# Softmax denominators in four column tiles, spread back by transfers, in a fused two-layer attention kernel

## The chip, the cores and the metric

The kernel runs on one core of a Trainium2 chip. The metric is the device time of one execution in microseconds; the number reported is the median of several. One profiled execution gives the trace from which all durations come.

## The reference

Two layers run one after the other on x, eight images of 512 channels and 32x32 = 1024 positions, all in float32. The change lies in the first layer. Cut to what matters here:

```python
h = _group_norm(x, gn_w, gn_b)                       # 32 groups of 16 channels
qkv = einsum('oc,bcn->bon', qkv_w, h) + qkv_b        # 8 heads of 64 channels
attn = einsum('bhdi,bhdj->bhij', q, k) * 64 ** -0.5
attn = softmax(attn, axis=-1)
out = einsum('bhij,bhdj->bhdi', attn, v)
out = einsum('oc,bcn->bon', proj_w, out) + proj_b
x = x + out
```

The second layer ranks the 1024 tokens of each image by their squared norm, normalizes the 256 largest and lets them attend to each other, writes the result back into the values, projects, and adds x again.

## The kernel before

**Tiling.** Layer 0 is cut into 64 units. A unit t is a pair of heads (p = t // 2, four pairs an image) and one half of the 1024 queries (512 of them), so eight units make an image b, and `at` = t % 8 is the unit's place in it. Keys lie on partitions: the scores of a unit come as eight tiles j of 128 keys by (2 heads x 512 queries). A softmax over keys is thus a reduction over partitions and over j.

**Steps of a unit.** Each is a small function, named in SLOT by a word:

- sc (L943): two matmuls, one per head, into a PSUM tile of two banks. keep (ACT, L951) copies it to SBUF (e); max (DVE, L957) folds it into a running maximum.
- turn (PE, L966): eight transposes of that maximum; neg (DVE, L971) reduces them to one negated maximum per query; spread (PE, L980) transposes it back over all partitions (ns).
- sub (DVE, L986) adds ns to e; exp (ACT, L989); add (POOL, L994) sums the eight e tiles into es, seven adds a unit; val (PE, L1002) multiplies e with v, two heads in two column tiles of 64, accumulated over the eight j into one bank (av).
- den (`total`, PE, L1015): ones times es, which sums the 128 partitions. Two matmuls, one per head, each with 64 columns of ones and 512 queries, so that each head's sum stands on the 64 partitions on which av has that head. take (ACT, L1023) copies the sums to ri; inv (DVE, L1027) takes the reciprocal; div (DVE, L1033) multiplies av with it into o.
- fill and empty: work of other units beside the attention: projections of q and k (L740), the v values (L761), the output projection of the image before (L779), each a group of matmuls into the one bank g, emptied by ACT or, for the output projection, by DVE (L786), with a store of the result and a load of the next residual rows on SP. A unit has three fills; a unit with `at` 1 to 4 has two more, of the output projection.

**What sets the order.** PE, DVE, ACT and POOL each run their instructions in the order in which the program names them; there is no scheduler for them. SLOT is that order, written out by hand: in the loop over t each word calls its step for unit t, with + for unit t+1 and - for unit t-1. The text is the same for every slot, and a step without work there is left out. SP, which issues the loads and stores, follows its own queue, in which a DMA behind a waiting one waits too. A loop with NORM and NORM1 hangs the group norm of the next image on words of SLOT: the statistics (L655), two small matmuls with gmat that sum over channel groups (`mean_sum` L660, `variance_sum` L678), their copies out (`mean_take` L665, `variance_take` L683), the factors, and the application (L699, four an image).

**Buffers.** PSUM has eight banks: two tiles of two banks (tag s) go round among the eight sc tiles, pt of turn and den; one tile of two banks is ns; one bank is av, one is g. A new tile of tag s waits until the readers of the tile two before it are done. In the first two units of an image den's second bank also takes the group-norm sums of the next image. av has one buffer, so the first val of a unit waits for div of the unit before.

**Around the end.** At t = UNITS-3 `load_layer1` puts x of image 0 and the weights of layer 1 (4 MB) on SP. The last slots also do layer 1's first steps (token rows, token values, importance counts), and `begin_layer1` (L1082) and `finish` (L1100) close layer 0 with the last den and the last output projections. Layer 1 has orders of its own (BATCH, END), which the change leaves alone.

Of the kernel before, what the change touches and what calls it, by code (L numbers as in the profile page):

```python
# [9 lines left out]
F32 = mybir.dt.float32  # L10
# [8 lines left out]
P = 128  # L19
B = 8  # L20
C = 512
N = 1024
CT = C // P
NB = N // P
NH = 2
HALF = N // NH
HEADS = 8
HD = 64
NPAIR = HEADS // 2
# [8 lines left out]
XT = 4  # L38
# [5 lines left out]


SLOT = """
take- sc0+ sc1+ spread inv- empty0 keep1+ fill1 keep0+ sub1 sub0 val6- exp1 sc2+ max1+
exp0 sc3+ sub3 div- empty1 sub7 sub4 fill2 keep2+ max3+ exp3 val0 max2+ val1 exp7 exp4
add1 add3 keep3+ add4 sub5 val3 sc4+ sc5+ empty2 fill3 exp5 val7 add7 empty3 sub2 keep5+
val5 max4+ val4 max5+ sub6 fill4 keep4+ empty4 add5 exp2 sc6+ max6+ exp6 sc7+ add2 keep6+  # L50
max7+ add6 keep7+ fill0+ turn+ den neg+ val2
"""


# [62 lines left out]
def attention_then_topk_attention(  # L117
# [18 lines left out]
    nc = tc.nc  # L136
# [33 lines left out]
    keep_pool = ctx.enter_context(tc.tile_pool(name="r1", bufs=2))  # L170
# [425 lines left out]
    def layer0():  # L596
        with ExitStack() as st:
# [6 lines left out]
            ap = st.enter_context(tc.tile_pool(name="ap", bufs=2))  # L604
# [90 lines left out]
            def norm_apply(b, c):  # L695
# [8 lines left out]


            NORM = {
                (-3, "max", 7): [(norm_stats, 0)], (-2, "div", 0): [(norm_stats, 1)],
                (-1, "div", 0): [(norm_stats, 2)], (0, "div", 0): [(norm_stats, 3)],
                (0, "neg", 0): [(mean_take,), (spread_of,)], (1, "neg", 0): [(variance_take,)],
                (2, "max", 7): [(norm_factors,)],  # L710
                (3, "sub", 5): [(norm_apply, c) for c in range(CT)],
            }

            NORM1 = {
                (-1, "max", 3): [(norm_stats, 0), (norm_stats, 1)],
                (-1, "max", 7): [(norm_stats, 2), (norm_stats, 3)],
                (3, "div", 0): [(norm_apply, 0)], (3, "sub", 5): [(norm_apply, 1)],
                (3, "sub", 6): [(norm_apply, 2)], (3, "max", 7): [(norm_apply, 3)],
            }

            def norms(t, name, j):
                for b in {t // (NPAIR * NH) + 1, (t + 3) // (NPAIR * NH) + 1}:
                    at = t - (b - 1) * NPAIR * NH
                    if 0 < b < B:
                        todo = NORM.get((at, name, j), [])
                        if b == 1 and name != "neg" and at != 2:
                            todo = NORM1.get((at, name, j), [])
                        for step, *which in todo:
                            step(b, *which)


            def project(p, which, hf):

                b, hp = divmod(p, NPAIR)
                all_ = (qs, ks)[which]
                ot = which * CT + hp

                def fill(pq):
                    for k in range(CT):
                        nc.tensor.matmul(  # L740
                            pq, wqkv[:, k, ts(ot, P)], hs[b][:, k, ts(hf, HALF)],
                            start=(k == 0), stop=(k == CT - 1),
                        )

                def empty(pq):
                    if hf == 0:
                        all_[p] = qp.tile([P, N], F32, tag="qk"[which], name=f"{'qk'[which]}_{p}")
                    nc.scalar.activation(
                        all_[p][:, ts(hf, HALF)], pq, AF.Identity, bias=bqkv[:, ot : ot + 1],
                    )  # L750

                return fill, empty
# [243 lines left out]
            def values(t, j):  # L996
# [4 lines left out]
                for hh in range(2):  # L1001
# [3 lines left out]
                        e[:, hh, :], start=(j == FIRST), stop=(j == LAST),  # L1005
                    )

            def total(t, _):
                den = ps_s.tile([P, 2, HALF], F32, tag="s", name=f"den_{t}")
                b, at = divmod(t, NPAIR * NH)  # L1010
                if b + 1 < B and at < 2:
                    (mean_sum, variance_sum)[at](b + 1, den[:, 1, :])
                es = sums.pop(t)
                for hh in range(2):
                    nc.tensor.matmul(  # L1015
                        den[HD * hh : HD * hh + HD, 0, :], ones0[:, :HD], es[:, hh, :],
                        start=True, stop=True,
                    )
                dens[t] = den

            def take(t, _):
                ri = ap.tile([P, HALF], F32, tag="ri", name=f"ri_{t}")
                nc.scalar.copy(ri, dens[t][:, 0, :])  # L1023
                dens[t] = ri

            def invert(t, _):
                nc.vector.reciprocal(dens[t], dens[t])  # L1027

            def divide(t, _):
                p, hf = divmod(t, NH)  # L1030
# [80 lines left out]
            with tc.manual_schedule(engines=ORDERED):  # L1111
                for c in range(CT):
                    norm_stats(0, c)
                mean_sum(0, ps_g.tile([P, HALF], F32, tag="g", name="pm_0"))
                mean_take(0)
                spread_of(0)
                variance_sum(0, ps_g.tile([P, HALF], F32, tag="g", name="pv_0"))
                variance_take(0)
                norm_factors(0)
                for c in range(CT):  # L1120
                    norm_apply(0, c)

                FIRST_STEPS = {
                    ("sc", 1): project(0, 0, 1), ("sc", 3): v_tokens(0, 0), ("sc", 5): v_tokens(0, 1),
                    ("keep", 0): "empty", ("keep", 3): "empty", ("keep", 4): "empty",
                }
                pending = []

                def first(step):
                    if step == "empty":  # L1130
                        end, pt = pending.pop(0)
                        end(pt)
                    else:
                        pool, tag = ((ps_g, "g"), (ps_a, "av"))[len(firsts) % 2]
                        firsts.append(step)
                        pt = pool.tile([P, HALF], F32, tag=tag, name=f"first_{len(firsts)}")
                        step[0](pt)
                        pending.append((step[1], pt))

                firsts = []  # L1140
                for step in (
                    project(0, 1, 0), project(0, 0, 0), "empty", project(0, 1, 1), "empty", "empty",
                ):
                    first(step)
                for t in range(-1, UNITS + 1):
                    b, at = divmod(t, NPAIR * NH)
                    if t == -1:
                        hs[1] = load_x(1)
                    if 0 <= t and at == CT + 1 and b + 2 < B:
                        hs[b + 2] = load_x(b + 2)  # L1150
                    if b == B - 1 and at == 0:
                        pair = tiles["pair"] = xp.tile([P, CT, N], F32, tag="x0", name="pair")
                        for i, src in enumerate((wvT, woT)):
                            nc.sync.dma_start(
                                pair[:, :, ts(i, C)], src.rearrange("(k p) o -> p k o", p=P)
                            )
                    if t == 2:
                        constants()
                    if t == UNITS - 3:
                        load_layer1()  # L1160
                    if 0 < b < B and 1 <= at <= CT:
                        for hf in range(NH):
                            load_residual(b - 1, at - 1, hf)
                    if t == UNITS - 1:
                        for mt in range(3):
                            load_residual(B - 1, mt, 0, spare(f"xr_last_{mt}")[:, :HALF])
                    for name, ahead, j in order:
                        if 0 <= t + ahead < UNITS and (name, t) != ("den", UNITS - 1):
                            STEPS[name](t + ahead, j)
                        if t == -1 and (name, j) in FIRST_STEPS:  # L1170
                            first(FIRST_STEPS[name, j])
                        norms(t, name, j)
                        if t == UNITS - 4 and name == "empty" and j == 4:
                            fill(t, 5)
                        if t == UNITS - 4 and (name, j) == ("exp", 6):
                            empty(t, 5)
                        if t == UNITS - 1 and (name, j) == ("fill", 1):
                            also(token_rows(1))
                            also(token_rows(2))
                    if t == UNITS - 1:  # L1180
                        begin_layer1()
                finish()
# [48 lines left out]
```

## Time and profile before

| | us |
|---|---|
| median of 3 runs | 2642.75 (2640.84 to 2644.28) |
| the profiled execution | 2641.48 |
| its span (first to last instruction) | 2639.8 |
| one image in the steady stretch | 258 |
| an ordinary unit of three fills (den to den, 1019.29 to 1047.90) | 28.6 |
| layer 0 ends, layer 1 begins at about | 2156 |
| reciprocal, DVE, 64 times | 3.352 each |
| copy of the sums, ACT, 64 times | 0.586 each |
| add, POOL, 448 times | 2.38 each |

How to read the lines further down: a group line has the line of the program, engine, operation, output and inputs, shape and count; then busy time and mean duration in ns; then the idle time ahead of it and what ended it. A timeline line has start, length, engine, line and operation, and in brackets the idle time ahead. A line of the table by stretch has the stretch, its length, and for PE, PE's weight loads, DVE, ACT and POOL the busy time (and the count); then the granted TensorE clock as a share of full speed, the share of the DMA engines' time, and GB/s.

TensorE's matmuls are pipelined, and the ends of its records are modelled. The start of one group to the start of the next is the better measure of what a group costs.

### The profile page before, as it was taken

The page shows a single profiled execution, that of the slowest core. Times are in us where ns is not written, and L with a number is a line of the kernel's source. Part 1 is how long each engine was busy: PE and PEld are TensorE (multiplying, and loading weights), DVE is VectorE, ACT ScalarE, POOL GpSimd, SP SyncE. Part 2 cuts the span into 40 slices and gives each one's busy share as a digit, 9 for nine tenths or more (in the row PEclk, how much of TensorE's full clock was granted, in tenths as well). Part 3 has the DMA queues.
Part 4 walks back from the last instruction along what each step waited for, and adds up shares of the span by engine and source line. Part 5 has one row for each costly group of instructions (what it writes and reads, how often), then busy time and mean ns, then how long its engine had stood idle before and what let it go on. Part 6 is the DMA issues. An engine that isn't in the chain of part 4 may idle for free. (4 is left out here: it accounts for less than half of the span.)

```text
span 2639.8 us, 27404 instructions
## 1 busy us (share of the span) xinstructions
PE 2586.0 (98%) x9932; PEld 1190.0 (45%) x9932; DVE 1920.2 (73%) x2434; ACT 1354.1 (51%) x1700; POOL 1161.1 (44%) x557
## 2 busy tenths in 40 slices
PE   7999999999999999999999999999999999999998
PEld 4444444444444444444444444444443345555554
DVE  5688868886878678867877787777767556666583
ACT  3556655665566456644665465556555433333421
POOL 1456644555455455544564465546544511211122
PEclk9999999999999999999999999999999999999999
DMA  3000001000100010001000100010002243555564
GB/s 132 1 7 30 1 24 56 17 1 32 57 9 1 32 64 1 1 32 64 0 1 32 64 1 9 24 64 1 15 26 88 76 176 116 199 202 206 195 207 140
DMA packets 78278, 158.58 MB, mean 60 GB/s; under 512 B 11946, under 2 KB 11946, under 8 KB 78144
## 3 DMA queue, kind: packets, MB, share of 16 engines
q1 hardware_dynamic: 52480, 113.27, 12.3%
q10 hardware_dynamic: 18144, 31.48, 3.2%
q0 software_dynamic: 7520, 12.09, 1.6%
q8 instruction: 79, 1.29, 0.2%
q14 instruction: 55, 0.45, 0.1%
HBM read 100.16 MB, written 69.21 MB: 64 GB/s over the span
## 5 line engine op out<-in xcount | busy, mean ns | idle before, releaser
L994 POOL TENSOR_TENSOR es<-es,e 128x1024 f32<-128x1024 f32 x384 | 913.1, 2378 | 346.8 <-ACT e L989 326.1
L951 ACT COPY e<-sc 128x1024 f32<-128x1024 f32 x512 | 508.1, 1013 | 568.4 <-PE sc L943 308.6
L986 DVE TENSOR_TENSOR e<-e,ns 128x1024 f32<-128x1024 f32 x512 | 603.5, 1205 | 2.5 <-PE ns L980 2.2
L989 ACT ACTIVATE e<-e 128x1024 f32<-128x1024 f32 x512 | 531.4, 1056 | 115.2 <-DVE e L986 108.6
L957 DVE TENSOR_TENSOR high<-sc,high 128x1024 f32<-128x1024 f32 x384 | 469.4, 1222 | 123.0 <-PE sc L943 59.1
L943 PE MATMUL sc<-q,k 64*128 64x512 f32 x2048 | 509.6, 615 | 4.8 <-DVE high L957 1.8
L1002 PE MATMUL av<-e,v 128*64 128x512 f32 x2048 | 492.7, 602 | 0.0
L994 POOL TENSOR_TENSOR es<-e,e 128x1024 f32<-128x1024 f32 x64 | 151.4, 2366 | 706.0 <-ACT e L989 706.0
L740 PE MATMUL g<-x,wqkv 128*128 128x512 f32 x992 | 453.0, 599 | 0.0
L943 PEld LDWEIGHTS sc<-q,k 64*128 64x128 f32 x2048 | 176.0, 186 | 328.9 <-issue 180.4
L740 PEld LDWEIGHTS g<-x,wqkv 128*128 128x128 f32 x992 | 178.5, 190 | 228.0 <-issue 224.2
L1002 PEld LDWEIGHTS av<-e,v 128*64 128x64 f32 x2048 | 130.0, 136 | 301.1 <-issue 294.7
L1027 DVE RECIPROCAL ri<-ri 128x512 f32<-128x512 f32 x64 | 214.6, 3352 | 26.3 <-ACT ri L1023 25.9
L761 PE MATMUL g<-wqkv,x 128*128 128x256 f32 x992 | 230.5, 385 | 0.0
L779 PE MATMUL g<-o,wp 128*128 128x512 f32 x472 | 221.3, 612 | 2.7 <-ACT V L313 2.7
L761 PEld LDWEIGHTS g<-wqkv,x 128*128 128x128 f32 x992 | 183.4, 190 | 68.0 <-issue 44.7
L299 PE MATMUL b_pv<-w,x 128*128 128x512 f32 x448 | 201.9, 598 | 0.0
L971 DVE TENSOR_REDUCE nm<-pt 128x8 f32<-128x1024 f32 x64 | 78.4, 1224 | 146.8 <-PE pt L966 146.8
L786 DVE SCALAR_TENSOR_TENSOR xr<-g,pb,xr 128x512 f32<-128x512 f32 x56 | 41.9, 749 | 170.9 <-PE g L779 170.9
L779 PEld LDWEIGHTS g<-o,wp 128*128 128x128 f32 x472 | 85.9, 192 | 134.7 <-issue 113.2
L524 POOL DMA_INDIRECT V<-sa,at x64 | 64.0, 1001 | 149.4 <-DMA sa<-att 54.6
L1023 ACT COPY ri<-den 128x512 f32<-128x512 f32 x64 | 37.5, 586 | 178.6 <-PE den L1015 135.1
(168 smaller groups left out, 2004.3 us busy)
## 6 DMA issues: line engine op xcount, KB each, us to landing
x<-in_x_dram SPq DMA_DIRECT2D x32, 512.0 KB, 5.2
x<-x1d SPq DMA_DIRECT2D x32, 512.0 KB, 6.2
sx<-xT ACTq DMA_DIRECT2D x64, 256.0 KB, 3.5
y<-x1d SPq DMA_DIRECT2D x64, 256.0 KB, 4.4
out_dram<-y SPq DMA_DIRECT2D x64, 256.0 KB, 3.4
xr<-in_x_dram SPq DMA_DIRECT2D x58, 256.0 KB, 2.5
x1d<-xr SPq DMA_DIRECT2D x58, 256.0 KB, 2.0
sv<-V ACTq DMA_DIRECT2D x56, 256.0 KB, 3.7
```

What stands on the lines that cost most here:

```text
L299: nc.tensor.matmul(pv, x1[b][:, k, ts(j, P)], w["vo"][:, k, :], start=(k == 0), stop=(k == CT - 1),)
L740: nc.tensor.matmul(pq, wqkv[:, k, ts(ot, P)], hs[b][:, k, ts(hf, HALF)], start=(k == 0), stop=(k == CT - 1),)
L761: nc.tensor.matmul(pv[:, ts(j, 2 * P)], hs[b][:, k, ts(2 * part + j, P)], wqkv[:, k, 2 * C + hm * 2 * P : 2 * C + (hm + 1) * 2 * P], start ...
L779: nc.tensor.matmul(po, wp[:, k, ts(mt, P)], os[b * NPAIR + k][:, ts(hf, HALF)], start=(k == 0), stop=(k == CT - 1),)
L943: nc.tensor.matmul(sc[:, hh, :], ks[p][r, ts(j, P)], qs[p][r, ts(hf, HALF)], start=True, stop=True,)
L951: nc.scalar.copy(raw[t, j], banks["s", t, j])
L957: nc.vector.tensor_tensor(high[t], banks["s", t, j], raw[t, 0] if j == 1 else high[t], ALU.max)
L986: nc.vector.tensor_tensor(raw[t, j], raw[t, j], high[t], ALU.add)
L989: nc.scalar.activation(raw[t, j], raw[t, j], AF.Exp, scale=QK_SCALE)
L994: nc.gpsimd.tensor_add(sums[t], raw[t, 0] if j == 1 else sums[t], raw[t, j])
L1002: nc.tensor.matmul(avs[t][HD * hh : HD * hh + HD, :], vs[p // 2][:, j, (p % 2) * P + HD * hh : (p % 2) * P + HD * hh + HD], e[:, hh, :], s ...
L1027: nc.vector.reciprocal(dens[t], dens[t])
```

## The change

Three things are done at once.

1. den is computed in four column tiles of 32 columns: a head's 512 queries are split into two halves of 256, and each (head, half) has a tile of its own. The sums thus stand as 128 partitions by 256 queries, each repeated over 32 partitions. take and inv work on 256 columns instead of 512. Their layout no longer fits av, so inv is followed by eight transfers on SP, each of 32 partitions by 256 queries (32 KB), that write the reciprocals into ri, 128 by 512. The sums' copy rs uses the buffers of tag xT, of which there are four.
2. In the units that carry a group-norm sum, the den tile is allocated and the small matmul issued ahead of turn, not at den.
3. SLOT gets a new order, and NORM, NORM1, FIRST_STEPS and one place at the end are hung on other words. den is now the last step of a slot, behind the last val; no val of a unit is left for the next slot; the order of the j's changes; mean_take and variance_take come after take instead of ahead of it.

```diff
 SLOT = """
-take- sc0+ sc1+ spread inv- empty0 keep1+ fill1 keep0+ sub1 sub0 val6- exp1 sc2+ max1+
-exp0 sc3+ sub3 div- empty1 sub7 sub4 fill2 keep2+ max3+ exp3 val0 max2+ val1 exp7 exp4
-add1 add3 keep3+ add4 sub5 val3 sc4+ sc5+ empty2 fill3 exp5 val7 add7 empty3 sub2 keep5+
-val5 max4+ val4 max5+ sub6 fill4 keep4+ empty4 add5 exp2 sc6+ max6+ exp6 sc7+ add2 keep6+
-max7+ add6 keep7+ fill0+ turn+ den neg+ val2
+take- sc0+ keep0+ inv- sc1+ spread max1+ sub0 keep1+ fill1 sub1 sub3 sub7 exp0 sc3+ empty1 div-
+sc2+ fill2 exp1 keep3+ exp7 sub6 max3+ val0 sub5 keep2+ val1 exp3 empty2 max2+ val7 exp5 add1
+fill3 sc5+ empty3 sc4+ fill4 add7 sub4 exp6 val3 add3 exp4 max5+ max4+ add5 val5 add4 keep5+
+val6 sc7+ sub2 keep4+ add6 empty4 keep7+ sc6+ exp2 max6+ fill0+ max7+ keep6+ empty0+ turn+ add2 val2
+neg+ val4 den
 """
...
             NORM = {
-                (-3, "max", 7): [(norm_stats, 0)], (-2, "div", 0): [(norm_stats, 1)],
-                (-1, "div", 0): [(norm_stats, 2)], (0, "div", 0): [(norm_stats, 3)],
-                (0, "neg", 0): [(mean_take,), (spread_of,)], (1, "neg", 0): [(variance_take,)],
-                (2, "max", 7): [(norm_factors,)],
-                (3, "sub", 5): [(norm_apply, c) for c in range(CT)],
+                (-3, "max", 7): [(norm_stats, 0)], (-2, "max", 7): [(norm_stats, 1)],
+                (-1, "sub", 2): [(norm_stats, 2)], (-1, "max", 7): [(norm_stats, 3)],
+                (1, "take", 0): [(mean_take,), (spread_of,)], (2, "take", 0): [(variance_take,)],
+                (2, "neg", 0): [(norm_factors,)],
+                (3, "max", 2): [(norm_apply, 0), (norm_apply, 1)],
+                (3, "empty", 4): [(norm_apply, 2), (norm_apply, 3)],
             }
...
+            def room(t):
+                return ps_s.tile([P, 2, HALF], F32, tag="s", name=f"den_{t}")
+
             def total(t, _):
-                den = ps_s.tile([P, 2, HALF], F32, tag="s", name=f"den_{t}")
-                b, at = divmod(t, NPAIR * NH)
-                if b + 1 < B and at < 2:
-                    (mean_sum, variance_sum)[at](b + 1, den[:, 1, :])
+                den = dens.pop(t) if t in dens else room(t)
                 es = sums.pop(t)
-                for hh in range(2):
+
+                for g in range(4):
+                    hh, c = divmod(g, 2)
                     nc.tensor.matmul(
-                        den[HD * hh : HD * hh + HD, 0, :], ones0[:, :HD], es[:, hh, :],
-                        start=True, stop=True,
+                        den[ts(g, P // 4), 0, : HALF // 2], ones0[:, : P // 4],
+                        es[:, hh, ts(c, HALF // 2)], start=True, stop=True,
                     )
                 dens[t] = den
 
             def take(t, _):
+                rs = keep_pool.tile([P, C], F32, tag="xT", name=f"rs_{t}", bufs=XT)
+                nc.scalar.copy(rs[:, : HALF // 2], dens[t][:, 0, : HALF // 2])
+                dens[t] = rs
+
+            def invert(t, _):
+
+                rs = dens[t]
+                nc.vector.reciprocal(rs[:, : HALF // 2], rs[:, : HALF // 2])
                 ri = ap.tile([P, HALF], F32, tag="ri", name=f"ri_{t}")
-                nc.scalar.copy(ri, dens[t][:, 0, :])
+                for r in range(4):
+                    for c in range(2):
+                        nc.sync.dma_start(
+                            ri[ts(r, P // 4), ts(c, HALF // 2)],
+                            rs[ts(r // 2 * 2 + c, P // 4), : HALF // 2],
+                        )
                 dens[t] = ri
-
-            def invert(t, _):
-                nc.vector.reciprocal(dens[t], dens[t])
...
                     for name, ahead, j in order:
+                        if name == "turn" and t >= 0 and at < 2 and b + 1 < B:
+                            dens[t] = room(t)
+                            (mean_sum, variance_sum)[at](b + 1, dens[t][:, 1, :])
                         if 0 <= t + ahead < UNITS and (name, t) != ("den", UNITS - 1):
                             STEPS[name](t + ahead, j)
```

More of the change, by code (lines that the diff above doesn't have):

```diff
@@ L706, in layer0 @@
             NORM = {
-                (-3, "max", 7): [(norm_stats, 0)], (-2, "div", 0): [(norm_stats, 1)],
-                (-1, "div", 0): [(norm_stats, 2)], (0, "div", 0): [(norm_stats, 3)],
-                (0, "neg", 0): [(mean_take,), (spread_of,)], (1, "neg", 0): [(variance_take,)],
-                (2, "max", 7): [(norm_factors,)],
-                (3, "sub", 5): [(norm_apply, c) for c in range(CT)],
+                (-3, "max", 7): [(norm_stats, 0)], (-2, "max", 7): [(norm_stats, 1)],
[4 more added lines that the diff above has]
+                (3, "empty", 4): [(norm_apply, 2), (norm_apply, 3)],
             }
             NORM1 = {
-                (-1, "max", 3): [(norm_stats, 0), (norm_stats, 1)],
+                (-1, "max", 2): [(norm_stats, 0), (norm_stats, 1)],
                 (-1, "max", 7): [(norm_stats, 2), (norm_stats, 3)],
-                (3, "div", 0): [(norm_apply, 0)], (3, "sub", 5): [(norm_apply, 1)],
-                (3, "sub", 6): [(norm_apply, 2)], (3, "max", 7): [(norm_apply, 3)],
+                (3, "sub", 6): [(norm_apply, 0)], (3, "max", 2): [(norm_apply, 1)],
+                (3, "sub", 2): [(norm_apply, 2)], (3, "max", 7): [(norm_apply, 3)],
             }
@@ L725, in norms @@
                         todo = NORM.get((at, name, j), [])
-                        if b == 1 and name != "neg" and at != 2:
+                        if b == 1 and at not in (1, 2):
                             todo = NORM1.get((at, name, j), [])
@@ L1123, in layer0 @@
                 FIRST_STEPS = {
-                    ("sc", 1): project(0, 0, 1), ("sc", 3): v_tokens(0, 0), ("sc", 5): v_tokens(0, 1),
-                    ("keep", 0): "empty", ("keep", 3): "empty", ("keep", 4): "empty",
+                    ("sc", 1): project(0, 0, 1), ("sc", 2): v_tokens(0, 0), ("sc", 4): v_tokens(0, 1),
+                    ("keep", 1): "empty", ("keep", 2): "empty", ("keep", 4): "empty",
                 }
@@ L1174, in layer0 @@
                             fill(t, 5)
-                        if t == UNITS - 4 and (name, j) == ("exp", 6):
+                        if t == UNITS - 4 and (name, j) == ("exp", 2):
                             empty(t, 5)
```

## The prediction

> **What bounds the kernel now.** I read the page's busy shares first, then a table of busy time by stretch, then the timeline of single units, then the queue of SP.
>
> ```profile
> PE 2586.0 (98%) x9932; PEld 1190.0 (45%) x9932; DVE 1920.2 (73%) x2434; ACT 1354.1 (51%) x1700; POOL 1161.1 (44%) x557
> 578.00:836.00 258.00, 258.00 (x998) 112.49 (x996) 202.04 (x187) 145.84 (x160) 133.23 (x57) 1.00 0.07 25
> L1015 PE MATMUL den<-es,ones 128*64 128x512 f32 x256 | 69.0, 617 | 1.5 <-POOL es L994 1.4
> ```
>
> In the steady stretch (one batch image, eight units, 258 us) TensorE is busy for all 258 us; DVE has 56 us to spare. So inside layer 0 a microsecond of TensorE is a microsecond of time, and work taken from DVE alone brings nothing. What one unit's end looks like, first in an ordinary unit, then in one that also carries a group-norm sum:
>
> ```profile
> 1046.93 1.04 PE L966 MATMUL pt<-ident,high 128*128 128x128 f32 x8
> 1047.90 1.08 PE L1015 MATMUL den<-es,ones 128*64 128x512 f32 x4
> 1048.81 1.03 PE L1002 MATMUL av<-e,v 128*64 128x512 f32 x4
> 1049.02 0.59 ACT L1023 COPY ri<-den 128x512 f32<-128x512 f32 x1 [2.77 <-PE den L1015]
> 1049.76 1.99 PE L943 MATMUL sc<-q,k 64*128 64x512 f32 x8
> ...
> 1105.23 1.08 PE L1015 MATMUL den<-es,ones 128*64 128x512 f32 x4
> 1106.14 1.03 PE L1002 MATMUL av<-e,v 128*64 128x512 f32 x4
> 1106.36 0.16 DVE L665 COPY gm<-den 128x4 f32<-128x4 f32 x1
> 1106.55 0.59 ACT L1023 COPY ri<-den 128x512 f32<-128x512 f32 x1 [3.09 <-DVE gm L665]
> 1107.10 1.99 PE L943 MATMUL sc<-q,k 64*128 64x512 f32 x8
> ```
>
> See three things. Starts of PE groups, not their lengths, are TensorE time: the denominators hold it from 1047.90 to 1048.81, 0.91 us for four records. A 512-column f32 matmul is two records; weight loads of a steady group come every 0.43 us, so a full-width matmul takes 0.85 us, and the two 64-column denominator tiles together take that of one: they run side by side. Third, the two readers of the den tile take turns: ACT's copy waits 3.09 us for DVE's gm, although both wait for PE only.
>
> Last, the queue of SP and the granted clock near the end of layer 0:
>
> ```profile
> 2019.02 1.75 SPq L207 DMA_DIRECT2D x<-x1d  x4
> 2021.57 1.33 SPq L217 DMA_DIRECT2D w<-in_wkT_dram  x1
> w<-in_wkT_dram SPq DMA_DIRECT2D x1, 1024.0 KB, 12.0
> 2099.45 6.77 PE L779 MATMUL g<-o,wp 128*128 128x512 f32 x8 [2.69 <-ACT V L313]
> 2100.00:2104.00 4.00, 4.00 (x6) 1.47 (x5) 0.91 (x1) 3.70 (x4) 3.84 (x3) 0.50 0.17 66
> ```
>
> 4 MB start at 2019.0 and the last lands at 2021.57+12.0 = 2033.6. And after 2.69 us of TensorE idleness the clock is granted at 0.50, so that a 3.6 us group takes 6.7.
>
> **What the Trainium skill says.** "TensorE: Matmul & The Clock Gate", Part 3: matmuls in different column groups run concurrently; three 32-column tiles gave 2.38x. The trace agrees for two 64-column tiles (0.91 us for both); no run shows four. The same page, Part 1: the clock is halved after idling; agrees (0.50 above). "TensorEngine Tiling (Array Packing)", Key Properties: changing the tiling mode drains the array. Agrees: eight scores records take 1.92 us where 4 x 0.427 = 1.71 would do, three av steps 2.73 for 2.56; a switch costs 0.1 to 0.2 us. "DMA: Bandwidth & Descriptors", Anatomy of one DMA: a DMA's semaphore wait is taken by the issuing sequencer; so what stands behind it on SP waits too. No row here isolates that.
>
> **The change part by part.** Times are against the profiled execution (span 2639.8, 2641.5 with what lies around it; the median of the runs is 1.3 higher).
>
> *Denominator matmuls.* Four 32-column tiles of 256 columns, if all side by side, take 2 x 0.213 = 0.43 us instead of 0.85. The mode switches: before, den shared its mode with val2, but val6 stood alone; after, den stands alone and val6 is in a group of three. Count of switches is 11 in a unit with three fills, before and after. So -0.43 us a unit; unit 63's den isn't on TensorE's path, so 63 x 0.427 = -26.9 us. Bounds: no less than 0.35 a unit gained if a switch of this new mode costs 0.08 more; nothing gained if only pairs run together.
>
> *Copy, reciprocal.* Half the columns: ACT 586 to some 370 ns (slope to the 1013 ns of 1024 columns), DVE 3352 to 1680. Both are off the bound: 0 by themselves. But before, val2 stood between den and the next scores; now den is directly ahead of them. With den starting at T, its last record ends near T+0.60 (a record ends 0.38 after the last one of 256 columns starts, as in L761's 385 ns), the copy starts at T+0.65 (0.05 after, as above), ends T+1.02. In ordinary units the second scores need it: they come at T+0.59+0.85 = 1.44. Hidden, 0.4 to spare.
>
> *Units with a group-norm sum* (two per image for seven images: 14). The den tile is now allocated ahead of pt, so the first scores, not the second, take its banks, and the mean's copy comes after ACT's. The listing of the changed program shows the chain: gm waits for ACT, the first scores wait for DVE. Copy ends T+1.02, gm starts 0.03 later and takes 0.16: T+1.21; scores start 0.06 to 0.14 after (54.36 after a DVE end at 54.30; 2028.41 after 2028.27), T+1.3 instead of T+0.59. Nothing else is in TensorE's queue: +0.7 each, 14 x 0.7 = +9.8 us (6 to 13).
>
> *Eight transfers and div.* The reciprocal ends 2.1 us after the first scores start. SP issues every 0.44 us (4 in 1.75 us), a small load lands in 1.6 to 1.8 (the 2 KB ln vectors): 2.1+8x0.44+1.8 = 7.4 us. DVE has max1 and four subtractions ahead of div (5 x 1.21 from 2.2): 8.2. Behind div wait four more DVE steps that release sc4's banks; val0 needs div at 11.8. So the transfer is hidden by up to some 2 us; eight waits on DVE at 51 ns each (the PE event rows) are too. What stands ahead on SP: the stores and residual loads of the unit before (the last store follows empty4, some 10 us before the unit's end, and lands in 2.0, the load behind it in 2.5), and in an image's fifth unit 2 MB of x, which wait for fill1 and are issued near 6.5 us of the unit before, so landed by its 20th. Both are clear of the transfers. Cost 0.
>
> *New order.* I walk a three-fill unit with these durations, from the start of its first scores. TensorE: two scores 1.92, ns 0.93, fill1 3.53, scores to 8.3, fill2 (the v step, 3.65) to 11.8, three av 2.73, scores, three av, scores to 21.1, fill0 to 24.6, turn 0.97, two av 1.87, den from 27.4. DVE and ACT: max1 3.4, sub0 4.6, exp0 5.7, empty1 7.3, sub7 8.2, div 8.9, max2 13.9, exp6 15.3, max4 18.2, keep4 19.2, max7 23.7. No step of TensorE comes late: fill2 at 8.3 needs empty1; sc4 at 15.5 max2; sc6 at 20.1 keep4; turn at 24.6 max7; den at 27.4 the last POOL add at 25.1 (seven of 2.37 behind exp2 at 22.5); neg ends 1.3 after turn, before den does. In the five-fill units fill4 (20.05) needs the DVE store step at 19.1. norm_apply (2.02 us each) falls into DVE's wait for fill3. Cost 0, or up to 0.1 a unit (+6) where I misjudge one.
>
> *The layer-1 loads.* The eight transfers of unit 60 stand behind the 4 MB on SP, and each waits for the transfer eight before it: the last for wk, 2033.6. It lands near 2035.5, div ends 2036.3. TensorE would be at val0 at 2022.3+9.9 = 2032.2: +4.1 us (2 to 6), and the clock may drop: +3, taken as +2.
>
> *The last two units.* A 1.23 us wait of den for POOL (2088.49) goes: -1.2. val6 moves ahead of the last units' sums: +0.7. The last div is 4.1 us after inv starts; with transfers 1.7+3.6+1.8+0.7 = 7.8, and DVE's counts stand behind: +3.6, less some 1 that later waits for DMA absorb: +2.5. Startup 0.
>
> Sum: -26.9 + 9.8 + 4.1 + 2 - 1.2 + 0.7 + 2.5 = -9.0 us, so 2632.5 for the profiled execution and 2633.8 against the median. I say 2633.5.
>
> **Rivals.** *A, most of it arrives.* The 14 waits are shorter (PE's queue absorbs them, or the copy is released sooner) and the clock doesn't drop: -26.9+3+4.1+2 = -18, 2625, at best 2616 if the tail costs nothing. For: TensorE is at 100% and nothing else is near. Against: the wait of scores on DVE is in the listing.
> *B, nothing to see.* Small waits in the new order, 0.1 a unit, and the tail at its upper ends: -9+6+4, 2643. For: several margins are below 1 us. Against: before ran with equally thin ones without a wait.
> *C, slower.* The four f32 tiles don't run side by side. Its place is the den group, its price 63 us for each us that den takes over 0.43; from 0.57 us on the gain is gone. At 0.85 (pairs) the time is -9+26.5 = +17.5, 2660. For: four tiles need sixteen weight loads and matmul records in 0.43 us and four moving streams, which no row shows. Against: the pairs overlap fully.
>
> **How the numbers follow.** Forecast (2625 to 2637) 0.44, A 0.22, B 0.13, C 0.21. What a measurement can tell from no change is about 0.2%, 5.3 us. Faster by more: the forecast and A, 0.66; within: most of B, 0.12; slower: C and the end of B, 0.22. The range 2615 to 2655 takes in A's best and C up to den at 0.77 us; the likeliest case's own is 2625 to 2640.
>
> **What would show it.** Right: den's group to the next group's start 0.5 to 0.6 us; in 14 units 0.6 to 0.8 us of PE idle ended by DVE gm or rs_ve ahead of sc; one wait of some 4 us of av on DVE's div near 2032; the 258 us of an image falling to about 256. Wrong: den at 0.8 or more; av waiting for div in every unit (ri landing later than 11 us after the first scores); waits of fills for ACT.

## The result, and the profile after

| | before | after |
|---|---|---|
| median of the runs, us | 2644.31 (2640.84 to 2645.41, 6 runs) | 2621.34 (2617.79 to 2626.22, 6 runs) |
| ratio to before | | 0.9919, 95% interval 0.9909 to 0.9929 |
| the profiled execution, us | 2641.48 | 2618.26 |
| its span, us | 2639.8 | 2616.5 |

The change saves 23 us, 0.8%; the forecast was a saving of 9. From the two traces, starts of the `turn` group (pt) against each other, which divides layer 0 into its slots:

| stretch | before | after | difference |
|---|---|---|---|
| up to the first pt | 52.01 | 51.17 | -0.84 |
| slots 0 to 7 | 249.11 | 246.07 | -3.04 |
| slots 8 to 55, six images | 6 x 258.14 | 6 x 254.73 | -20.4 |
| an ordinary unit of three fills | 28.61 | 28.17 | -0.44 |
| slots 56 to 62 | 236.27 | 237.39 | +1.12 |
| last pt to the first b_pt of layer 1 | 69.70 | 72.89 | +3.19 |
| layer 1, b_pt to the end of the span | 483.88 | 480.58 | -3.3 |

The change leaves the code of layer 1 alone, and over the eleven traces of this case layer 1 takes 477.6 to 483.9 us, so its 3.3 us are taken for a difference between executions. That isn't shown: there is one trace of before, and its 483.9 is the longest of the eleven. Of the 3.3, 1.7 us is clock: at the start of layer 1 it is at one half for 6.8 us in before and for 3.4 us in after.

Busy shares on the page of after, the den group in its list of groups, then the table by stretch of the same kernel (stretch, PE, PE's weight loads, DVE, ACT, POOL, granted clock, DMA share, GB/s):

```profile
PE 2556.5 (98%) x10188; PEld 1184.6 (45%) x10188; DVE 1813.0 (69%) x2434; ACT 1347.5 (52%) x1700; POOL 1159.1 (44%) x557
```

```profile
L1018 PE MATMUL den<-es,ones 128*32 128x256 f32 x512 | 40.9, 391 | 0.0
```

```profile
574.00:830.00 256.00, 256.00 (x1036) 112.55 (x1034) 189.93 (x188) 146.02 (x161) 134.05 (x57) 1.00 0.11 34
```

TensorE is still busy for all of the steady stretch; the unit is shorter because the TensorE work is. Next the timeline of after, the end of an ordinary unit:

```profile
1033.27 1.04 PE L967 MATMUL pt<-ident,high 128*128 128x128 f32 x8
...
1034.24 1.94 PE L1003 MATMUL av<-e,v 128*64 128x512 f32 x8
...
1036.10 0.64 PE L1018 MATMUL den<-es,ones 128*32 128x256 f32 x8
1036.67 1.99 PE L944 MATMUL sc<-q,k 64*128 64x512 f32 x8
1036.81 0.37 ACT L1026 COPY rs<-den 128x256 f32<-128x256 f32 x1 [2.65 <-PE den L1018]
...
1037.21 1.75 DVE L1032 RECIPROCAL rs<-rs 128x256 f32<-128x256 f32 x1 [1.65 <-ACT rs L1026]
...
1038.99 4.95 SPq L1036 DMA_DIRECT2D ri<-rs  x8
...
1045.45 0.69 DVE L1046 TENSOR_TENSOR o<-av,ri 128x512 f32<-128x512 f32 x1 [0.76 <-issue]
```

From the start of den to the start of the scores it is 0.57 us. The chain behind it, copy, reciprocal, eight transfers, div, ends 9.5 us after the first scores have started (1046.14 against 1036.67); no matmul of the steady stretch waits for it. And the end of a unit that carries a group-norm sum:

```profile
1089.60 0.28 PE L660 MATMUL den<-mv,gmat 128*128 128x4 f32 x2
...
1092.61 0.64 PE L1018 MATMUL den<-es,ones 128*32 128x256 f32 x8
...
1093.18 1.99 PE L944 MATMUL sc<-q,k 64*128 64x512 f32 x8
1093.32 0.37 ACT L1026 COPY rs<-den 128x256 f32<-128x256 f32 x1 [2.83 <-PE den L1018]
1093.72 0.16 DVE L665 COPY gm<-den 128x4 f32<-128x4 f32 x1 [1.65 <-ACT rs L1026]
...
1093.94 0.40 PEld L944 LDWEIGHTS sc<-q,k 64*128 64x128 f32 x4 [0.46 <-DVE gm L665]
...
1095.10 1.09 PE L981 MATMUL ns<-ident,nm 128*128 128x128 f32 x8
```

den to scores is 0.57 us here too. DVE's gm does wait for ACT's copy, as foreseen. But it is a weight load in the middle of the group, that of the second scores, which waits for gm; it comes 0.06 us after gm's end, and the group lasts 1.92 us to ns (1093.18 to 1095.10), just as it did in the kernel before. The first scores start at 1093.18, ahead of the copy that reads den (1093.32), so they don't write den's banks.

By the rule given under Buffers, that a tile takes the place of the tile two before it, they would have to. In the kernel before, where pt comes ahead of den, that rule gives the right banks; in these units of after it doesn't. The addresses in the built program have den, allocated ahead of pt, in the same two banks as the second scores, and pt in those of the first.

Last, where layer 0 ends, in after: the queue of SP, the only two waits of TensorE for div, and the clock (table by stretch).

```profile
1991.98 1.75 SPq L207 DMA_DIRECT2D x<-x1d  x4
...
1993.78 0.71 SPq L217 DMA_DIRECT2D w<-in_wqT_dram  x1
1994.53 0.64 SPq L217 DMA_DIRECT2D w<-in_wkT_dram  x1
1997.51 9.16 SPq L1036 DMA_DIRECT2D ri<-rs  x8
...
2008.18 0.69 DVE L1046 TENSOR_TENSOR o<-av,ri 128x512 f32<-128x512 f32 x1 [4.97 <-DMA ri<-rs]
...
2008.92 4.44 PE L1003 MATMUL av<-e,v 128*64 128x512 f32 x12 [3.79 <-DVE o L1046]
...
2119.72 0.69 DVE L1046 TENSOR_TENSOR o<-av,ri 128x512 f32<-128x512 f32 x1 [6.58 <-DMA ri<-rs]
...
2120.47 11.43 PE L780 MATMUL last<-o,wp 128*128 128x512 f32 x26 [3.25 <-DVE o L1046]
```

```profile
2010.00:2020.00 10.00, 10.00 (x28) 3.29 (x24) 6.31 (x6) 4.02 (x5) 2.68 (x2) 0.83 0.00 0
```

A queue line joins issues of one kind and shows the time from the first to the last. The eight transfers of this unit take 9.16 us to issue, with the layer-1 loads ahead of them; elsewhere they take 4.95. Six of them are issued at the usual pace, by 2001.21; the seventh comes at 2002.97 and the eighth at 2006.16. Counted eight places back, as the prediction counts, these two stand behind wq and wk. div waits 4.97 us and av 3.79 behind it, and then the clock drops: 0.83 is the mean of 10 us of which 3.4 are at 0.50, and a group of twelve av records takes 4.44 us where 2.79 is usual. At the very end the last output projection waits 3.25 us for the last div.

### The profile page after: what moved, and what is told of

Read it like the earlier page. It is cut to its first block, busy times and chain, and to the rows that moved or that the text cites. A ratio compares the mean times of both kernels' runs of the same rounds, so it can differ in the third digit from the quotient of the medians.

```text
span 2616.5 us, 28723 instructions
## 1 busy us (share of the span) xinstructions
PE 2556.5 (98%) x10188; PEld 1184.6 (45%) x10188; DVE 1813.0 (69%) x2434; ACT 1347.5 (52%) x1700; POOL 1159.1 (44%) x557
## 5 line engine op out<-in xcount | busy, mean ns | idle before, releaser
L952 ACT COPY e<-sc 128x1024 f32<-128x1024 f32 x512 | 517.3, 1011 | 357.2 <-PE sc L944 198.2
L1003 PE MATMUL av<-e,v 128*64 128x512 f32 x2048 | 483.3, 603 | 3.8 <-DVE o L1046 3.8
L762 PEld LDWEIGHTS g<-wqkv,x 128*128 128x128 f32 x992 | 183.4, 190 | 67.9 <-ACT e L990 44.7
L1032 DVE RECIPROCAL rs<-rs 128x256 f32<-128x256 f32 x64 | 112.0, 1750 | 69.1 <-ACT rs L1026 69.1
L299 PEld LDWEIGHTS b_pv<-w,x 128*128 128x128 f32 x448 | 82.8, 191 | 91.2 <-issue 90.9
L395 PE MATMUL b_pp<-w,selT 128*128 128x512 f32 x256 | 112.8, 595 | 0.9 <-ACT selT L386 0.7
```

The lines of the kernel that those rows point to most:

```text
L299: nc.tensor.matmul(pv, x1[b][:, k, ts(j, P)], w["vo"][:, k, :], start=(k == 0), stop=(k == CT - 1),)
L395: nc.tensor.matmul(pp, tiles["selT", b][:, k, ts(rb, P)], w["qk"[which]][:, k, :], start=(k == 0), stop=(k == CT - 1),)
L762: nc.tensor.matmul(pv[:, ts(j, 2 * P)], hs[b][:, k, ts(2 * part + j, P)], wqkv[:, k, 2 * C + hm * 2 * P : 2 * C + (hm + 1) * 2 * P], start ...
L952: nc.scalar.copy(raw[t, j], banks["s", t, j])
L1003: nc.tensor.matmul(avs[t][HD * hh : HD * hh + HD, :], vs[p // 2][:, j, (p % 2) * P + HD * hh : (p % 2) * P + HD * hh + HD], e[:, hh, :], s ...
```

## The experiments

Four ran together with before on one chip, four on another occasion, one alone with before. Each ratio is to the runs of before beside it (medians 2639.7, 2639.35 and 2638.99 us). The ratios are those on record; they aren't the quotients of the medians and differ from them by up to 0.0007, some 2 us.

| kernel | median, us | ratio | 95% interval | ordinary unit, us |
|---|---|---|---|---|
| before | 2639.7 | 1 | | 28.61 |
| after, again | 2617.18 | 0.9911 | 0.9895 to 0.9926 | 28.17 |
| group-norm sums at den | 2620.63 | 0.9925 | 0.9912 to 0.9939 | 28.17 |
| layer-1 loads behind the transfers | 2611.96 | 0.9899 | 0.9884 to 0.9915 | 28.17 |
| new order, old den | 2638.64 | 1.0000 | 0.9991 to 1.0008 | 28.45 |
| old order, new den | 2631.05 | 0.9972 | 0.9962 to 0.9983 | 28.32 |
| sixteen transfers | 2882.23 | 1.0927 | 1.0912 to 1.0941 | 31.5 to 33.5 |
| loads behind, last unit old | 2607.18 | 0.9883 | 0.9868 to 0.9898 | 28.17 |
| no transfers | 2604.39 | 0.9871 | 0.9856 to 0.9886 | 28.17 |
| den's matmuls twice | 2644.36 | 1.0020 | 1.0012 to 1.0028 | 28.60 |

### After once more

> The changed kernel once more, as the yardstick for the runs beside it. Both theories: 2618 to 2626 us, about 23 us below the kernel before. If the spread of some 8 us between its runs comes from the granted clock after TensorE's two long waits near the end (2008 and 2120 us), the slow runs have a lower mean clock (0.993 against 0.996).

2617.18 us (2612.51 to 2620.5): on this chip, too, 22 to 23 us below before. It is the yardstick for the three that ran with it. The units of its trace agree with those of after to 0.02 us until slot 60; slot 60 to 61, with the wait at the layer-1 loads, is 39.85 us in it and 38.87 in after. The spread of after's own six runs goes with the clock, as was expected: the three above 2623 us have a mean clock of 0.992 to 0.993, the three below 2619 us 0.994 to 0.996, and 0.003 of 2617 us is 8 us.

### Where the group-norm sums stand

```diff
-                        if name == "turn" and t >= 0 and at < 2 and b + 1 < B:
+                        if name == "den" and t >= 0 and at < 2 and b + 1 < B:
```

> One part undone: the den tile of a unit with a group-norm sum is allocated, and the small matmul issued, at den and not ahead of turn. Theory of the prediction: the early allocation gave the first scores den's banks and cost 14 x 0.7 us that I then failed to see; without it 9 to 10 us faster than the changed kernel, about 2611. Theory after the trace: the first scores took the banks that neg frees, so the place costs only one more change of tiling (the small matmul is full width, between two column-tiled groups): 14 x 0.1 to 0.3 us slower, +1 to +4 us.

3.4 us slower than after, by medians whose intervals overlap; the trace is sharper. Per image the units with `at` 0, 1 and 2 take 28.17 + 35.75 + 35.74 us, in after 28.31 + 35.60 + 35.46: 0.29 more, 2 us for seven images. den to scores is 0.57 us in both. So what this part of the change saves is a little TensorE time, and there was no 0.7 us wait to be had back by undoing it: the step of the forecast that put 9.8 us on it is wrong.

### The layer-1 loads behind the transfers of their slot

```diff
-                    if t == UNITS - 3:
-                        load_layer1()
...
                     for name, ahead, j in order:
...
+                        if t == UNITS - 3 and name == "inv":
+                            load_layer1()
```

> The layer-1 loads (4 MB) are issued behind unit 60's eight transfers instead of ahead of them. Theory that these transfers wait behind the loads: the 3.79 us wait of av for div near 2008 and the slow clock after it (4.44 us for a 2.79 us group) go, 5 to 6 us faster than the changed kernel, about 2614. Rival, that the wait only moves on (the loads land later and token_values waits for them, or the next wait takes its place): within 1.5 us of the changed kernel.

5.2 us below after, as the first theory said; the two intervals still overlap a little, and the trace decides. The queue and the timeline of this kernel:

```profile
1991.95 1.75 SPq L207 DMA_DIRECT2D x<-x1d  x4
...
1997.48 4.97 SPq L1036 DMA_DIRECT2D ri<-rs  x8
2002.49 0.58 SPq L217 DMA_DIRECT2D w<-in_wqT_dram  x1
2003.12 0.51 SPq L217 DMA_DIRECT2D w<-in_wkT_dram  x1
...
2003.77 0.69 DVE L1046 TENSOR_TENSOR o<-av,ri 128x512 f32<-128x512 f32 x1 [0.59 <-DMA ri<-rs]
...
2005.03 2.79 PE L1003 MATMUL av<-e,v 128*64 128x512 f32 x12
```

The four x loads still start early; the two weights now follow the transfers. The eight issue in 4.97 us as anywhere else, av waits for nothing and takes its usual 2.79 us. Slot 60 to 61 falls from 38.87 to 33.36 us: the wait and the clock drop behind it cost 5.5 us, and the two weights ahead in the queue are what caused them.

### The new order with the old den

```diff
-                for g in range(4):
-                    hh, c = divmod(g, 2)
+                for hh in range(2):
                     nc.tensor.matmul(
-                        den[ts(g, P // 4), 0, : HALF // 2], ones0[:, : P // 4],
-                        es[:, hh, ts(c, HALF // 2)], start=True, stop=True,
+                        den[HD * hh : HD * hh + HD, 0, :], ones0[:, :HD], es[:, hh, :],
+                        start=True, stop=True,
                     )
```

Copy and reciprocal are the old ones too, and there are no transfers.

> The new order with the old denominators: two tiles of 64 columns, 512 queries, the reciprocal in place, no transfers. Theory that the tiles bring the gain: 0.44 us a unit come back (+28), while the waits for transfers at the end go (-5 to -9): 2636 to 2643, within 8 us of the kernel before. Rival, that the new order brings most of it: 2625 or less.

No difference from before that can be told. Its timeline, to be held against the ordinary unit of after above:

```profile
1047.24 1.94 PE L1003 MATMUL av<-e,v 128*64 128x512 f32 x8
1049.00 1.03 PE L1017 MATMUL den<-es,ones 128*64 128x512 f32 x4
1049.96 1.99 PE L944 MATMUL sc<-q,k 64*128 64x512 f32 x8
```

From the av group to the scores it is 2.72 us here and 2.43 in after: 0.29 less with four tiles. The ordinary unit is 28.45, so the order by itself saves 0.16 there. But the units with `at` 0, 1 and 3 take 28.60, 36.28 and 36.26 us where before took 28.61, 35.99 and 35.87; over an image the order saves 0.05 us (258.09 against 258.14). In a unit with `at` 1 the trace shows why:

```profile
850.25 3.35 DVE L1029 RECIPROCAL ri<-ri 128x512 f32<-128x512 f32 x1
...
853.51 1.16 DVE L958 TENSOR_TENSOR high<-sc,e 128x1024 f32<-128x1024 f32 x1
...
855.04 1.01 ACT L952 COPY e<-sc 128x1024 f32<-128x1024 f32 x1 [3.96 <-DVE high L958]
...
856.91 0.68 ACT L749 ACTIVATE q<-g,bqkv 128x512 f32<-128x512 f32 x1
...
857.65 3.72 PE L762 MATMUL g<-wqkv,x 128*128 128x256 f32 x16 [0.35 <-ACT q L749]
```

DVE comes to max only behind the reciprocal, ACT's copy waits for max, the step that empties fill1 (q) stands behind that copy on ACT, and fill2 waits for it. With the reciprocal of 1.75 us, in after, the same fill2 comes in time. In the unit with `at` 3 fill4 waits in the same way for a step of DVE (0.3 us). So the excess comes from the longer reciprocal in this order; with the old order the length of the reciprocal costs nothing, as the next run shows.

### The old order with the new den

SLOT, NORM and the place of the group-norm sums are those of before; den, take, inv and the transfers are those of after.

> The order of before (SLOT, NORM and the place of the group-norm sums) with the four column tiles and the transfers of after. Theory 'the tiles bring the gain, the order little': an ordinary unit of 28.61 us loses 0.40 to 0.45 of den and misses at most the 0.15 that the new order alone brought (28.45): 28.2 to 28.35 us, and the end of layer 0 waits for transfers as in after (+4.5, +3). The time is 0 to 8 us above after. Rival 'the order is there for the transfers': div stands earlier in the old order and its wait for the transfers reaches TensorE in every unit, 0.5 us or more of idle each; the time is then 30 us or more above after, slower than before.

2631.05 us: of the expected kind, though more than the 8 us above after that were allowed. The ordinary unit has 28.32 us, inside what was expected, and of the units only the one behind the layer-1 loads waits for div. An image takes 255.83 us against 254.73 in after, 6.6 us over six images; slots 56 to 62 take 241.69 against 237.39, 41.12 of them from slot 60 to 61, where the layer-1 loads cost more in this order. So order and tiles depend on each other: the order is worth nothing without the tiles, and 14 us by the medians (measured on two occasions) together with them, of which the traces place 9.4 in layer 0 from the first pt on. They don't depend on each other in the ordinary unit, where the order saves 0.16 us without the tiles and 0.15 with them, but in the units with `at` 1 and 3 and at the layer-1 loads.

### den's matmuls twice

```diff
-                for g in range(4):
-                    hh, c = divmod(g, 2)
+                for g in (0, 1, 2, 3, 0, 1, 2, 3):
+                    hh, c = divmod(g, 2)
```

> The four den matmuls issued twice over, into the same banks; no other tiling comes in between, so it gives the price of the four tiles without the switches around them. Theory 'all four run side by side at 0.427 us and the switch to their tiling is separate, 0.14 us': den to the first scores 0.57 + 0.43 = 1.00 us, an ordinary unit 28.17 + 0.43 = 28.60, 63 x 0.43 = +27 us against after, about as slow as before. Rival 'the group of 0.57 us is the tiles themselves, the switch costs nothing': +0.57 a unit, +36 us. Rival 'the records hide part': +0.3 or less a unit, +19 us or less.

```profile
1048.27 1.94 PE L1003 MATMUL av<-e,v 128*64 128x512 f32 x8
1050.14 1.07 PE L1018 MATMUL den<-es,ones 128*32 128x256 f32 x16
1051.14 1.99 PE L944 MATMUL sc<-q,k 64*128 64x512 f32 x8
```

27 us above after, as the first theory said. The timeline of this kernel has 1.00 us from den to scores, 0.43 more than after, and an ordinary unit of 28.60, again 0.43 more. So four tiles of 256 columns cost 0.43 us, what one such matmul would cost alone (two records of 0.213): all four run side by side. The other 0.14 us of the 0.57 is what is left for the switch between tilings, which wasn't varied by itself. It closes the sum of the unit in both orders: 28.61 - 0.43 (half the columns) + 0.14 (den has a tiling of its own now) = 28.32, what the old order has, and with 0.16 less for the order 28.16.

### Sixteen transfers for eight

```diff
                 for r in range(4):
-                    for c in range(2):
+                    for c in range(4):
                         nc.sync.dma_start(
-                            ri[ts(r, P // 4), ts(c, HALF // 2)],
-                            rs[ts(r // 2 * 2 + c, P // 4), : HALF // 2],
+                            ri[ts(r, P // 4), ts(c, P)],
+                            rs[ts(r // 2 * 2 + c // 2, P // 4), ts(c % 2, P)],
                         )
```

> Sixteen transfers of 32 partitions by 128 queries in place of eight of 256. Prediction's reading of the margin (val0 needs div 11.8 us after the first scores): at a pitch of 0.62 us the last of sixteen is issued some 5 us later, so div comes at 13.5 to 14 in place of 8.8, and av waits some 2 us in every unit; 63 x 2 is 125 us, less what the clock and POOL give or take: 100 to 200 us slower than after. Rival 'the transfers are far from the path': DVE's 7 us to spare a unit takes it up, the wait is below 0.5 us, under 30 us slower.

More than expected: some 265 us above after. A unit's timeline, and then the list of TensorE's waits (sum, number, longest):

```profile
1011.67 1.99 PE L944 MATMUL sc<-q,k 64*128 64x512 f32 x8
...
1014.90 10.02 SPq L1036 DMA_DIRECT2D ri<-rs  x16
...
1026.20 0.69 DVE L1046 TENSOR_TENSOR o<-av,ri 128x512 f32<-128x512 f32 x1 [5.73 <-DMA ri<-rs]
...
1026.94 2.79 PE L1003 MATMUL av<-e,v 128*64 128x512 f32 x12 [3.26 <-DVE o L1046]
```

```profile
PE av L1003 <- DVE o L1046: 181.8, 62, 8.4
```

TensorE was ready for the first av at 1026.94 - 3.26 = 1023.68, 12.0 us after the first scores: the forecast's point from which the transfers decide (11.8) was right, and in after div is done 2.5 us ahead of it. Half the bytes in each transfer don't make the issue cheaper: 10.02 us for sixteen, 4.95 for eight, 0.62 us apiece either way. The wait is 2.9 us in 62 units, 182 us of the 265, where the forecast had 2 us a unit. Most of the rest goes with the clock: its mean is 0.973 over the span of 2877.1 us where after has 0.996, by an estimate 2877 x 0.023 = 66 us.

### No transfers

```diff
-                nc.vector.tensor_mul(os[p][:, ts(hf, HALF)], avs.pop(t), dens.pop(t))
+                half = dens.pop(t)[:, : HALF // 2].unsqueeze(1).broadcast_to([P, 2, HALF // 2])
+                nc.vector.tensor_mul(
+                    os[p][:, ts(hf, HALF)].rearrange("p (a n) -> p a n", a=2),
+                    avs.pop(t).rearrange("p (a n) -> p a n", a=2), half,
+                )
```

The lines that issue the eight transfers are gone too.

> The eight transfers are left out; div multiplies both halves of a unit's queries with the same 256 reciprocals, so the output is not the reference's. It gives the price of all transfers together. Theory 'they cost only the wait at the layer-1 loads and the one at the last div': 5.5 + 3, with the clock, 7 to 10 us less than after, an ordinary unit still 28.15 to 28.2 us. Rival 'they cost a little in every unit' (DVE waits for them in 43 units, 1 us each): an ordinary unit 0.1 to 0.3 us shorter and 15 to 25 us less than after.

0.9871 against 0.9911 for after: all transfers together cost about 0.4%, 10.5 us by the ratios and 13 by the medians (the two didn't run side by side), more than the 7 to 10 expected. Ordinary units and the six middle images are the same to 0.01 us, so in the steady stretch the transfers cost nothing, and the waits of DVE that the trace of after lists for them (44.7 us in 43 units) are covered, but for the two at the end. By stages the cost lies in slots 56 to 62 (237.39 to 231.87 us), in the end (72.89 to 65.50), and, not expected, in slot 3 of the first image (31.52 to 29.24). There div comes 0.9 us later with the transfers, and DVE doesn't make up for it: TensorE's later waits in that slot end with DVE's maximum and ACT's copies.

### A faster version: loads behind, and the last unit with the old den

To the moved loads comes, for the last unit alone:

```diff
             def take(t, _):
+                if t == UNITS - 1:
+                    ri = ap.tile([P, HALF], F32, tag="ri", name=f"ri_{t}")
+                    nc.scalar.copy(ri, dens[t][:, 0, :])
+                    dens[t] = ri
+                    return
```

with total and invert as before the change in the same way.

> The layer-1 loads behind the transfers of their slot, as in the run before with that edit, and the very last unit with the old den (two tiles of 64 columns, copy and reciprocal of 512 columns in place, no transfers). Theory 'the end of layer 0 costs what the last div waits for': the 3.25 us wait of the last project_out goes, 2 to 4 us less than with the loads moved alone, 7 to 10 us less than after: about 0.9865 to 0.988 of before. Rival 'it waits for something else as well' (count, POOL, the reciprocal's 3.35 us in place of 1.75): 0 to 1 us less than with the loads moved alone.

```profile
2099.47 1.08 PE L1018 MATMUL den<-es,ones 128*64 128x512 f32 x4
...
2104.02 3.60 PE L299 MATMUL last<-w,x 128*128 128x512 f32 x8
...
2104.27 3.35 DVE L1043 RECIPROCAL ri<-ri 128x512 f32<-128x512 f32 x1
...
2107.45 13.90 PE L780 MATMUL last<-o,wp 128*128 128x512 f32 x32
...
2107.73 0.69 DVE L1060 TENSOR_TENSOR o<-av,ri 128x512 f32<-128x512 f32 x1
```

The output projection runs on without a break: the 3.25 us wait is gone although the reciprocal takes 3.35 us again. The end takes 66.29 us, where the five traces of the new order with eight transfers in the last unit have 71.7 to 73.7. With 2607.18 us, 0.9883, it is the fastest kernel here that leaves nothing out: 1.2% below before, 10 us below after's second measurement and 4.8 below the moved loads alone, a little more than the first theory said (both were measured on another occasion). Its interval lies below that of after's first measurement (0.9919) and overlaps that of the second by 0.0003.

## Why the prediction came out as it did

Its direction was right, and the time lay in the range; 2633.5 was 12 us too high for the 2621.34 that came, which lies outside the 2625 to 2640 of its likeliest case and nearer to its rival A, "most of it arrives" (2625, at best 2616). Rival A has the size by luck: its reasons, that the 14 waits are cut short and that the clock stays up, aren't what happened. Of the signs named, den's 0.57 us and the one wait of av (3.79) came; the 14 waits didn't, and an image fell to 254.7 us, not to about 256. The steps:

- **Denominator matmuls, -26.9.** Right, and for the reason given: four tiles side by side, with the count of switches the same before and after. The unit lost 0.44 us where 0.427 was said. Rival C, four tiles that don't overlap, is excluded by doubling them (+0.43 us).
- **Copy and reciprocal, 0.** Right; 0.37 and 1.75 us measured where 0.37 and 1.68 were put. In the old order their shortening brings nothing either way (an image loses eight times what an ordinary unit does, 2.31 us); in the new order it is needed, since the old reciprocal costs it 0.4 to 0.5 us in the units with `at` 1 and 3.
- **The 14 units with a group-norm sum, +9.8. This is the step that failed.** It said that "the first scores, not the second, take its banks". The trace has the second scores' weight load waiting for gm and the first waiting for nothing. The chain up to gm is as described, to 0.06 us, but it meets its consumer 0.76 us into the scores, when that is just due. The listing showed that the first scores wait for DVE, and the forecast took this for gm. It is neg: the first scores have pt's banks, neg is the reader of pt, and it is the last DVE instruction that ended before they start (at 1092.08). The three units around the sum cost 0.34 us an image over ordinary ones, against 0.24 in the kernel before: +0.7 in all. Without the 9.8 the sum is -18.8, 2624.
- **Eight transfers and div, 0.** Right for the steady stretch, with the margin right as well. Mis-sized: SP's issue is 0.62 us, not 0.44, which was taken from loads of x; a unit's last transfer thus leaves 1.4 us later than thought, and DVE, which was to be busy until then, waits for it in 43 units. Slot 3 of the first image pays 2.3 us, which the forecast didn't foresee.
- **New order, 0.** Right with the new den; the switch that it saves was counted with the matmuls.
- **Layer-1 loads, +4.1 and clock +2.** Right: 5.5 measured by moving the loads, wait (3.79) and clock (the rest) together. The clock's part differs between executions, as the last section shows.
- **The last two units, -1.2 + 0.7 + 2.5.** The wait for POOL went (-0.67 net in that slot), but the last div cost more than put: from the reciprocal's start to div's end it is 9.0 us (2111.40 to 2120.41), not 7.8, again by SP's issue. The end took 3.2 us more than before, where +2.5 was put.
- Between -18.8 and the -23.3 of the two traces 4.5 us are left, most of it 3.3 in layer 1 and 0.8 ahead of the first pt, which no part of the change explains. The medians differ by as much as the traces (23.0 and 22.5 us), so it stays open whether these are chance.

## What to carry to other kernels

Sums over partitions that must stand beside each other can be cut into column tiles until all column groups are used; on a kernel that TensorE bounds, it pays by the columns saved, less one switch of tiling, and an order that joins groups of one tiling elsewhere saves as much again (here 0.14 and 0.16 us a unit). A layout repair by small transfers was free here where its result was due later than number times issue time plus landing, and dear in two places: behind bulk loads in the same queue, and at the last unit, where nothing covers it; there the old form is better. A listing that shows a wait on an engine doesn't show on which instruction: look for the tile's last reader, and the next user of those very banks, before pricing it.

## What the runs showed of the hardware

- Issuing a transfer on SP took 0.62 us for 32 KB and for 16 KB alike.
- Four f32 column tiles of 32 columns by 256 took 0.43 us, fully side by side; entering a tiling of their own took 0.14, by difference.
- The clock is on record as full or as one half, the half in stretches of 3.4 us, 6.8 and in one run also 10.2. Whether it drops behind a wait of some 3 us isn't the same each time. One wait is in all eleven traces, that of the output projection for V, 2.7 to 2.8 us long: in six of them a stretch at one half begins in it or within 1.5 us of its end (before, after, its repeat, sums at den, new order with old den, sixteen transfers), in five none. The last projection's wait of 3.25 us was followed by full speed in after (11.43 us for 26 records); with the loads moved it was 3.26 us, and the same 26 records took 14.44, at a mean of 0.77 (2113 to 2127 us). Runs of one kernel differ by this; nothing here shows what decides it.
